# Queries of three more pairs by seven products of halves, with key/value units, sums of the input and a reload placed anew

## The chip, the cores and the metric

The kernel runs on one core of one Trainium2 chip. The metric is the device time of one execution in microseconds (us), the median of three runs. The profile comes from one further execution, taken by the hardware profiler.

Names used below: PE is TensorE's matmul, PEld its weight load, DVE is VectorE, ACT is ScalarE, POOL is GpSimd and SP is SyncE, whose queue issues nearly all transfers ("SPq"). In the trace every float32 matmul of the program appears as two records, so counts of records are twice the counts of matmuls in the code.

## The reference, cut to what matters

One layer over a sequence of S = 1024 tokens of width H = 512, all in float32, between two residual additions:

```python
# attention: 32 query heads, 8 key/value heads (groups), head size 128, causal
x = x + layernorm(attn(layernorm(x)))          # q, k, v, o projections, softmax over keys
# second half: dense 512 -> 512 with bias, plus 8 low-rank experts of rank 16
x = x + layernorm(ffn(layernorm(x)))           # router of 15 outputs, top 8, softmax weights
```

In `attn`, `q = xn @ w_q` has 4096 columns, that is 8 groups of 4 heads, and `k = xn @ w_k` and `v = xn @ w_v` have 1024 columns each, one head for each group. The changed lines concern `q`, and the places of `k` and `v`, for the last two of the eight groups.

## The kernel before

**Blocks.** The tokens are cut into 8 tiles of 128. A block (g, t) is the attention of one group g (four heads) for the queries of tile t; there are 64 blocks, numbered i = 0 to 63. Two consecutive blocks with tiles 2u and 2u+1 form a pair (g, u). Groups 0 to 5 take pairs 0 to 23 in order (blocks 0 to 47; the constant `N2` is 48). The last two groups are interleaved: pairs 24 to 31 are (6,0), (7,0), (6,3), (7,3), (6,2), (7,2), (6,1), (7,1), so blocks 48 to 53 are (6,0), (6,1), (7,0), (7,1), (6,6), (6,7), and block 54 is (7,6). A tile is finished once its block of group 7 is done; then come the output's norm, the router and the second half for that tile.

**One block.** The main loop goes through i. In each block `scores` runs four times (n = 0 to 3), each time on 128 rows (four heads of 32 queries): PE multiplies queries by keys into a PSUM tile `s` (a pool of two), DVE adds the mask (L618) and takes the negative maximum (L620), ACT takes the exponential into `p` (L625), DVE the reciprocal of the sum (L631), ACT scales `p` (L632), DVE transposes it in 32x32 squares into `T` (L638), and at the block's end SP issues 16 transfers from `T` to `K` (L109). Two blocks later `weighted_values` multiplies `K` by the values (`po`), and ACT copies the result to `attnT` (L669). After each of the four `scores` a quarter of the other matmul work of the block is emitted by `run_share`. That work is put together in `projections` and in the loop from: the queries of the next pair (`pq`), keys (`pk`), values (`pv` in the trace; in the loop the name `pv` holds the `po` pieces of block i-2), and the output projection of a finished pair by seven products (`pa` to `pe`), whose sums DVE adds up (L744). `weave` mixes two lists in proportion to their columns.

PE's order is the order in which the loop emits matmuls, since `keep` pins it; so one matmul that waits holds back all behind it. DVE, ACT, POOL and SP also work through queues in order.

**Queries in two ways.** `project_q` (L425 for its two copies by ACT) makes a pair's queries, 512 columns of `w_q` by 256 tokens, by 16 matmuls of 256 columns. `project_q_halves` makes the same by the seven products of a 2x2 scheme: the weights and the normed input `xnT` are cut into quarters, sums of quarters are made beforehand, and 28 matmuls of 128 columns follow, four for each product. The products lie in four PSUM banks (0 to 3, two products each, the last with one) and are put together by one ACT copy (L476) and six DVE additions (L450). Matmul banks come from a pool of three, so each bank must be emptied before the third bank after it is begun.

The sums are POOL's. `combine_q` (L145) makes four sums of quarters of `w_q` for one group, each 128x512, one of them in place in the weights, the others into three tiles tagged `hy`. `combine_x` (L188) makes four sums of quarters of `xnT` for one 256-token unit u, each 128x256, into two tiles tagged `x`, a pool of two: the sums of the next unit can't be written before the last matmul that reads the old ones. The same two buffers hold `xr`, the rows of x which `reload_x` brings back for the residual.

`QW` lists the pairs whose queries are made by halves: 2 to 24 before. Pairs 25 to 31 use `project_q`. The query weights of the last pairs alternate between groups 6 and 7 and have one buffer for each half (tags `wq0` and `wq1`), so at each even block `loads` issues two transfers of 512 KB on SP for the pair whose queries follow.

**Keys and values of the last two groups.** `project_k_halves` and `project_v_halves` make the keys and values of both groups for one unit u, 14 matmuls of 128 columns each. Unit 0 is made in block 47, units 1, 2 and 3 in blocks 49, 50 and 51 (n = 1, 2, 3 in `projections`). The keys are emitted ahead of the queries, the values go to `other`, which the loop weaves with the output projection and the values' products.

Of the kernel before, what the change touches and what calls it, by code (L numbers as in the profile page):

```python
# [22 lines left out]
def kernel(  # L23
# [36 lines left out]
    G = w_k.shape[1] // D  # L60
    R = w_q.shape[1] // D // G
    NT = S // P
# [6 lines left out]
    NSUB = P // SQ  # L69
    GV = 2  # L70
# [19 lines left out]
    blocks = [(g, 2 * u + e) for g, u in pairs for e in range(2)]  # L90
    N = len(blocks)
    N2 = (G - 2) * NT
    QW = range(2, N2 // 2 + 1)

    def keep(ins):
        return tc.keep_in_program_order(ins)
# [174 lines left out]
    def prepare_map():  # L271

        emap_f = const.tile([P, NR], F32, tag="emap_f", name="emap_f")
        keep(nc.vector.tensor_copy(emap_f, emap_i))
        for e in range(E):
            keep(
                nc.vector.tensor_scalar(
                    mexp[:, e, :], emap_f, float(e), SCALING, ALU.is_equal, ALU.mult
                )
            )  # L280
# [171 lines left out]
    def project_q_halves(m):  # L452


        g, u = pairs[m]
        hk = KC // 2
        pm = {}

        def half(e, h):

            return both(e)[:, h]

        def both(e):
            q = qTs[g, u][:, ts(e, NSUB), :, :]
            return q.rearrange("p s (x h) q -> p x s (h q)", x=2)

        def each(x):

            return qTs[g, u].rearrange("p s (x h) q -> p x s (h q)", x=2)[:, x]

        def merge(b):

            one, two = pm[b][:, 0], pm[b][:, 1]
            if b == 0:
                q = each(0).rearrange("p (e s) n -> p e s n", e=2)
                nc.scalar.copy(q, one.unsqueeze(1).to_broadcast([P, 2, NSUB, 2 * SQ]))  # L476
                add(half(0, 0), two, half(0, 0))
            elif b == 1:
                add(half(1, 0), one, half(1, 0))
                add(half(1, 1), two, half(1, 0))  # L480
            elif b == 2:
                add(half(0, 1), one, half(1, 1))
                add(half(1, 0), two, half(1, 0))
            else:
                add(both(1), one.unsqueeze(1).to_broadcast([P, 2, NSUB, 2 * SQ]), both(1))

        def piece(n, c, k):
            i, b, x = PRODUCTS[n], n // 2, n % 2
            if n == c == k == 0:
                qTs[g, u] = act.tile([P, PQ // SQ, R, SQ], F32, tag="qT", name=f"qT_{g}_{u}")  # L490
            if x == c == k == 0:
                whole = bank(f"pq_{g}_{u}_{b}")
                pm[b] = whole.rearrange("p (x s n) -> p x s n", x=2, s=NSUB)
            assert weights["sq"] == (g,) and weights["tx of"] == u
            matmul(
                pm[b][:, x, :, ts(c, SQ)],
                weights["sq", 0][i][:, k, ts(c, D)],
                weights["tx"][i][:, k, :].rearrange("p (s q) -> p s q", q=SQ),
                start=(k == 0),
                stop=(k == hk - 1),  # L500
            )
            if c == 1 and k == hk - 1 and (x == 1 or n == 6):
                merge(b)

        return [
            (P, lambda n=n, c=c, k=k: piece(n, c, k))
            for n in range(7)
            for c in range(2)
            for k in range(hk)
        ]  # L510
# [34 lines left out]
    def project_k_halves(g, u):  # L545
        def quarters():
            qb, at = u * PQ // QB, u * PQ % QB
            if at == 0:
                for n in (g, g + 1):
                    key_tile(n, qb)  # L550
            one, two = (kTs[n, qb][:, at : at + PQ] for n in (g, g + 1))
            return one[:, :P], one[:, P:], two[:, :P], two[:, P:], one.rearrange("p (e n) -> p e n", e=2)

        return project_halves(f"k{g}", u, ("sk", g), lambda w, x: (w, x), quarters)

    def project_v_halves(gv, u):
        def quarters():
            v = value_tile(gv, u)
            return v[:, 0, 0], v[:, 1, 0], v[:, 0, 1], v[:, 1, 1], v[:, :, 0]

        return project_halves(f"v{gv}", u, ("sv", gv), lambda w, x: (x, w), quarters)
# [204 lines left out]
    def reload_x(t):  # L766
        xt = state["x", t] = ffn.tile([P, H], F32, tag="x", name=f"xr_{t}")
        load(xt, x[ts(t, P), :])
# [118 lines left out]
    def projections(i):  # L887


        g, t = blocks[i]  # L890
        q, other = [], []
        m = i // 2 + 1
        if i == 0:
            later["q"] = project_q(*pairs[m])
            q = later["q"][: 2 * KC]
        elif i == 1:
            q = later["q"][2 * KC :]
        elif i % 2 and m < len(pairs):
            q = project_q_halves(m) if m in QW else project_q(*pairs[m])
        first = GV  # L900
        n = i - N2
        if i % 2 and m < len(pairs) and n < 0:
            gm, um = pairs[m]
            if gm >= first and gm % 2 == 0:
                q = project_k_halves(gm, um) + q + project_v_halves(gm // GV, um)
        if n < 0:
            if g < first and t == 2:
                other += project_k(g, 1)
            if g + 1 < first and t == 6:
                other += project_k(g + 1, 0)  # L910
            if g == 0 and t < 2:
                other += [(P * KC, lambda n=TPB + 2 + t: input_turn(n))]
                other += project_v(0, 2 + t)
            elif g == 0 and t >= TPB:
                other += project_v(0, t)
        elif 0 < n < NT // 2:
            q = project_k_halves(G - 2, n) + q
            other += project_v_halves((G - 2) // GV, n)
        return q, other

    def loads(i):
# [44 lines left out]
    def weave(a, b):  # L966

        na, nb = sum(c for c, _ in a), sum(c for c, _ in b)
        merged, at, bt, b = [], 0, 0, list(b)
        for c, f in a:  # L970
            merged.append((c, f))
            at += c
            while b and (bt + b[0][0] / 2) * na <= at * nb:
                bt += b[0][0]
                merged.append(b.pop(0))
        return merged + b
# [23 lines left out]
    def complete(i, *behind):  # L1000


        for e in range(2):
            k = i - behind[e % len(behind)]
            if 0 <= k < N and k % 2 == e and blocks[k][0] == G - 1:
                return [blocks[k][1]]
        return []
# [4 lines left out]
    ready = []  # L1012
    for i in range(N):
        loads(i)
        for t in complete(i, 2):
            reload_x(t)
        q, other = projections(i)
        pv = attend(i - 2) if i >= 2 else []
        o, o_pair, ends, begins = [], [], [], []
        for t in complete(i, 3):  # L1020
            o = project_o(*blocks[i - 3])
        if i % 2 == 0 and i >= 4 and blocks[i - 4][0] < G - 1:
            o_pair = project_o_pair(*pairs[i // 2 - 2])
        for t in complete(i, 6, 7):
            ends = sum(ffn_out(t), [])
        for t in complete(i, 5):
            begins = ffn_router(t)

        rest = o + weave(o_pair, other + pv[:2] + begins[1:] + pv[2:])

        if i % 2 and i // 2 + 1 in QW and blocks[i][1] > 1 and i > 3:
            cut = len(rest) * 3 // 5
            q, rest = weave(q, rest[:cut]), rest[cut:]
        then = begins[:1] + q + ends[:-1] + rest[:4] + ends[-1:] + rest[4:]
        for n in range(NSUB):
            scores(*blocks[i], n)
            run_share(then, n, NSUB)
            m = i // 2 + 1
            if i % 2 == 0 and m in QW:
                if n == 0:  # L1040
                    combine_x(pairs[m][1], m)
                if n == 1:
                    combine_q(m)
            g, t = blocks[i]
            if g % 2 and g + 1 < G and n == 1:
                if t == 6:
                    combine_k(g + 1)
                if t == 7:
                    combine_v((g + 1) // GV)
            if n == NSUB - 1 and i in (N2, N2 + 1, N2 + 2):  # L1050
                combine_x(i - N2 + 1, 0)
        if i == 1:
            combine_o(0)
        if i == NT:
            prepare_ffn()
        if i == NT + 4:
            prepare_map()
        ready += complete(i, 7, 8)
        for t in [t for t in ready if ("done", t) in state]:
            ready.remove(t)  # L1060
            ffn_store(t)

        if i >= NT and blocks[i - 2][1] == 0 and blocks[i - 2][0] < G - 1:
            combine_o(blocks[i - 2][0])
# [77 lines left out]
```

## Time and profile before

| | |
|---|---|
| three runs, us | 1066.48, 1066.59, 1067.16 (median 1066.59) |
| profiled execution: own time, span, us | 1066.64, 1064.9 |
| busy: PE, DVE, ACT, POOL, us | 1046.5, 740.1, 480.7, 255.0 |
| granted TensorE clock | 0.996 |

The span runs from the first instruction to the last; the profiled execution's own time is 1.7 us longer. A block can be found in the trace by its first score matmul, whose columns grow with the tile and the quarter: block 48 begins at 740.77 us, 49 at 753.71, 50 at 775.15, 51 at 789.77, 52 at 806.05, 53 at 818.64 and 54 at 837.25. In the chain of waits, each line says which engine's work stood on the path that ended last.

### The profile page before, as it was taken

Reading aid. Unit: us, or ns where it says so; the run is one execution under the profiler, and the core shown is the slowest. Engines: PE = TensorE matmul, PEld = TensorE weight load, DVE = VectorE, ACT = ScalarE, POOL = GpSimd, SP = SyncE. Lnnn points to the kernel's source line nnn. Section 1 sums busy time; section 2 is a strip of 40 time slices with the busy share of each in tenths; the row PEclk is TensorE's granted clock in tenths of the full one; section 3 lists DMA queues with packets and bytes.
Section 4 is the critical chain, followed back from the end, with each engine's and each line's share of the span. In section 5 each row is a group of like instructions: output and inputs, shape, how many; then the busy total and the mean of one; then the engine's idle time right before and its main releaser. Section 6 shows DMA issues by size and latency. Waiting matters only on the chain.

```text
span 1064.9 us, 15423 instructions
## 1 busy us (share of the span) xinstructions
PE 1046.5 (98%) x4782; PEld 729.8 (69%) x4782; DVE 740.1 (70%) x1810; ACT 480.7 (45%) x965; POOL 255.0 (24%) x491
## 2 busy tenths in 40 slices
PE   9999999999999999999999999999999999999996
PEld 7766667767777676767777667767787566466553
DVE  4586657876687766877577776887457766576756
ACT  3655435553344534553245544554235554353421
POOL 2613125241131215241130313351130110111212
PEclk9999999999999999999999999999999999999998
DMA  5146352563125442463225352464523754444231
GB/s 188 34 115 149 70 121 70 150 154 86 27 56 154 104 108 72 115 158 79 61 50 131 102 125 61 127 160 109 129 66 104 183 143 111 125 110 106 69 84 40
DMA packets 78513, 111.99 MB, mean 105 GB/s; under 512 B 18176, under 2 KB 49920, under 8 KB 78432
## 3 DMA queue, kind: packets, MB, share of 16 engines
q1 hardware_dynamic: 74960, 105.71, 39.5%
q0 software_dynamic: 2096, 3.46, 1.4%
q10 hardware_dynamic: 1376, 1.84, 0.5%
q8 instruction: 39, 0.64, 0.3%
q14 instruction: 42, 0.34, 0.1%
HBM read 33.34 MB, written 2.10 MB: 33 GB/s over the span
## 4 chain that ended last, share of the span: by engine, by line
PE 90%; DVE 3%; SPq 3%; ACT 1%; DMA 1%; issue 1%; POOL 0%; POOLq 0%; DVEq 0%; ACTq 0%
PE po L103 22%; PE s L103 20%; PE pq L103 19%; PE pv L103 5%; PE pe L103 4%; PE pa L103 4%; PE pk L103 4%; PE pf L103 3%; PE pO L103 3%; SPq L109 3%; PE pc L103 2%; PE pb L103 2%; PE pd L103 2%; PE pl L103 1%; DMA wo<-in_w_o_dram 1%
## 5 line engine op out<-in xcount | busy, mean ns | idle before, releaser
L632 ACT ACTIVATE p<-p,rec 128x32 f32<-128x32 f32 (+31 forms) x256 | 188.3, 736 | 225.8 <-DVE rec L631 164.8
L103 PE MATMUL po<-K,v 128*128 128x512 f32 x576 | 280.3, 594 | 1.7 <-DMA wo<-in_w_o_dram 1.0
L103 PE MATMUL s<-kT,qT 128*128 128x512 f32 (+15 forms) x768 | 272.4, 463 | 1.4 <-ACT p L625 1.3
L625 ACT ACTIVATE p<-s,nmax 128x32 f32<-128x32 f32 (+31 forms) x256 | 179.5, 701 | 163.1 <-DVE nmax L620 147.2
L638 DVE STREAM_TRANSPOSE T<-p 128x128 f32<-128x128 f32 (+7 forms) x256 | 197.7, 774 | 52.5 <-ACT p L632 37.9
L103 PEld LDWEIGHTS s<-kT,qT 128*128 128x128 f32 x768 | 141.2, 190 | 118.2 <-issue 105.9
L620 DVE TENSOR_REDUCE nmax<-s 128x1 f32<-128x32 f32 (+31 forms) x256 | 180.2, 704 | 7.3
L103 PEld LDWEIGHTS po<-K,v 128*128 128x128 f32 x576 | 103.6, 190 | 61.7 <-issue 51.4
L623 POOL MEMSET p<- 128x96 f32 (+2 forms) x192 | 29.3, 157 | 423.2 <-DVE T L638 377.5
L618 DVE TENSOR_TENSOR s<-s,smask 128x32 f32<-128x32 f32 x256 | 48.0, 187 | 99.4 <-PE s L103 98.8
L103 PE MATMUL pq<-xnT,wq 128*128 128x128 f32 (+1 forms) x656 | 113.3, 321 | 0.0
L103 PEld LDWEIGHTS pq<-xnT,wq 128*128 128x128 f32 x656 | 99.5, 191 | 14.0 <-issue 7.2
L188 POOL TENSOR_TENSOR tx<-xnT 128x256 f32<-128x256 f32 x52 | 37.9, 729 | 209.8 <-PE pv L103 124.6
L450 DVE TENSOR_TENSOR qT<-pq,qT 128x256 f32<-128x256 f32 x138 | 62.0, 460 | 32.0 <-ACT qT L476 18.9
L669 ACT COPY attnT<-po 128x512 f32<-128x512 f32 x64 | 37.4, 584 | 76.5 <-PE po L103 76.3
L103 PE MATMUL pa<-wo,attnT 128*128 128x256 f32 x224 | 58.8, 385 | 0.0
L103 PEld LDWEIGHTS pq<-tx,wq 128*128 128x128 f32 x368 | 47.1, 192 | 7.6 <-issue 7.5
L103 PEld LDWEIGHTS pq<-tx,sq 128*128 128x128 f32 x368 | 47.5, 192 | 5.7 <-issue 5.0
L103 PE MATMUL pq<-tx,sq 128*128 128x128 f32 x368 | 51.2, 275 | 0.0
L103 PEld LDWEIGHTS pa<-wo,attnT 128*128 128x128 f32 x224 | 41.0, 190 | 14.0 <-issue 9.3
L625 ACT ACTIVATION_READ_ACCUMULATOR p<-s,nmax 128x1 f32 x256 | 49.5, 193 | 0.0
L103 PE MATMUL pq<-tx,wq 128*128 128x128 f32 x368 | 49.2, 275 | 0.0
(146 smaller groups left out, 1258.4 us busy)
## 6 DMA issues: line engine op xcount, KB each, us to landing
K<-T SPq DMA_DIRECT2D x128, 128.0 KB, 2.4
K<-T SPq DMA_DIRECT2D x128, 112.0 KB, 2.3
wq<-in_w_q_dram SPq DMA_DIRECT2D x27, 512.0 KB, 4.8
K<-T SPq DMA_DIRECT2D x128, 96.0 KB, 2.2
K<-T SPq DMA_DIRECT2D x128, 80.0 KB, 2.1
wo<-in_w_o_dram SPq DMA_DIRECT2D x32, 256.0 KB, 3.9
K<-T SPq DMA_DIRECT2D x108, 64.0 KB, 2.0
K<-T SPq DMA_DIRECT2D x113, 48.0 KB, 2.0
```

The costliest lines, as they stand in the source:

```text
L103: keep(nc.tensor.matmul(*args, **kw))
L109: keep(by.dma_start(dst, src))
L188: nc.gpsimd.tensor_tensor(dst, p, q, ALU.subtract)
L450: nc.vector.tensor_tensor(dst, src, to, ALU.add)
L618: keep(nc.vector.tensor_tensor(s[:, n - SQ : n], s[:, n - SQ : n], smask, ALU.add))
L620: keep(nc.vector.tensor_reduce(nmax, s[:, :n], AX.X, ALU.max, negate=True))
L623: nc.gpsimd.memset(p[:, n:full], 0.0)
L625: keep(nc.scalar.activation(p[:, :n], s[:, :n], AF.Exp, bias=nmax, accum_out=total))
L632: keep(nc.scalar.mul(p[:, :n], p[:, :n], rec))
L638: nc.vector.transpose(turned[g, t][:, :, j, :, :].rearrange("p b k q -> p k b q"), p[:, :full].rearrange("p (k b q) -> p k b q", b=R, q=SQ),)
L669: copy = nc.scalar.copy(o, po)
```

## The change

`QW` is extended by three, to pairs 25, 26 and 27, which are (7,0), (6,3) and (7,3). Each of these needs sums of its weights, so `combine_q` now runs in blocks 48, 50 and 52, after the first quarter (n = 0) and not after the second.

The queries of pair 25 move from block 49 to block 48, and those of pair 27 from block 53 to block 52. In both blocks they stand at the end, behind the woven output projection and `po` work. Those of pair 26 stay in block 51. The sums of `xnT` of units 2 and 3 are emitted a quarter earlier. The keys and values of unit 1 stand in block 49 behind the first three `po` pieces, and those of units 2 and 3 stand ahead of the other work, the values no longer woven with the output projection. `reload_x`, and with it its transfer on SP, comes at the end of a block and not at its beginning. The query weights' transfers stay in the same blocks.

```diff
-    QW = range(2, N2 // 2 + 1)
+    QW = range(2, N2 // 2 + 4)
...
-        elif i % 2 and m < len(pairs):
+        elif i % 2 and m < len(pairs) and i not in (N2 + 1, N2 + 5):
             q = project_q_halves(m) if m in QW else project_q(*pairs[m])
...
         elif 0 < n < NT // 2:
-            q = project_k_halves(G - 2, n) + q
-            other += project_v_halves((G - 2) // GV, n)
+            kv = project_k_halves(G - 2, n), project_v_halves((G - 2) // GV, n)
+            if n == 1:
+                other += kv[0] + kv[1]
+            else:
+                q = kv[0] + q + kv[1]
+        elif n in (0, NT // 2):
+
+            other += project_q_halves(m)
         return q, other
...
         loads(i)
-        for t in complete(i, 2):
-            reload_x(t)
         q, other = projections(i)
...
         rest = o + weave(o_pair, other + pv[:2] + begins[1:] + pv[2:])
+        if i in (N2, N2 + NT // 2):
+            rest = weave(o_pair, pv) + other
+        if i == N2 + 1:
+            rest = pv[:3] + other + pv[3:]
...
             if i % 2 == 0 and m in QW:
-                if n == 0:
+                if n == 0 and i < N2:
                     combine_x(pairs[m][1], m)
-                if n == 1:
+                if n == (1 if i < N2 else 0):
                     combine_q(m)
...
-            if n == NSUB - 1 and i in (N2, N2 + 1, N2 + 2):
+            if (i, n) in ((N2, 3), (N2 + 1, 2), (N2 + 2, 2)):
                 combine_x(i - N2 + 1, 0)
...
+        for t in complete(i, 2):
+            reload_x(t)
         ready += complete(i, 7, 8)
```

## The prediction

> **What bounds the kernel now.** I read the page first. PE is busy for nearly the whole span and carries nine tenths of the chain that ended last.
>
> ```profile
> span 1064.9 us, 15423 instructions
> PE 1046.5 (98%) x4782; PEld 729.8 (69%) x4782; DVE 740.1 (70%) x1810; ACT 480.7 (45%) x965; POOL 255.0 (24%) x491
> ...
> PE 90%; DVE 3%; SPq 3%; ACT 1%; DMA 1%; issue 1%; POOL 0%; POOLq 0%; DVEq 0%; ACTq 0%
> ```
>
> So time is PE time plus whatever PE waits. Then I read PE's timeline over blocks 47 to 54 (start, length, engine, line, operation, count, and in brackets a wait). The first three lines are parts of the pair-24 products by halves (block 47), the next four the queries of pair 25 by full matmuls (block 49), the last the only wait of blocks 48 to 54.
>
> ```profile
> 730.70 1.06 PE L103 MATMUL pq<-xnT,sq 128*128 128x128 f32 x8
> 731.60 1.06 PE L103 MATMUL pq<-tx,sq 128*128 128x128 f32 x8
> 732.49 1.06 PE L103 MATMUL pv<-wv,xnT 128*128 128x128 f32 x8
> ...
> 757.11 1.89 PE L103 MATMUL pq<-xnT,wq 128*128 128x256 f32 x8
> 758.84 0.49 PE L103 MATMUL s<-kT,qT 128*128 128x192 f32 x2
> 759.16 5.34 PE L103 MATMUL pq<-xnT,wq 128*128 128x256 f32 x24
> 764.34 0.54 PE L103 MATMUL s<-kT,qT 128*128 128x224 f32 x2
> ...
> 784.22 0.49 PE L103 MATMUL pv<-wv,tx 128*128 128x128 f32 x2 [0.30 <-DVE acc L744]
> ```
>
> Lengths overlap, so cost is start to start: eight 128-column records take 0.89 us (731.60 to 732.49), 0.1115 each; 256-column records take 6.91 us for 32 (757.11 to 758.84 and 759.16 to 764.34), 0.216 each. The table of stretches gives each block's length and DVE's load in it; these are blocks 50, 52 and 53.
>
> ```profile
> 775.15:789.77 14.62, 14.32 (x96) 12.77 (x95) 10.38 (x36) 4.71 (x16) 3.20 (x7) 1.00 0.15 36
> ...
> 806.05:818.64 12.59, 12.59 (x47) 8.74 (x46) 11.25 (x23) 7.46 (x12) 0.30 (x2) 1.00 0.37 118
> 818.64:837.25 18.61, 18.61 (x62) 11.40 (x61) 14.19 (x22) 11.27 (x17) 0.61 (x4) 1.00 0.59 135
> ```
>
> Columns are length, then PE, PEld, DVE, ACT, POOL busy. POOL's and SP's timelines last: one set of weight sums takes 5.1 us, and SP's 16 transfers of a block stand 10 us ahead of the next weights.
>
> ```profile
> 706.17 1.27 POOL L145 TENSOR_TENSOR sq<-wq 128x512 f32<-128x512 f32 x1 [0.96 <-DMA wq<-in_w_q_dram]
> ...
> 709.98 1.27 POOL L145 TENSOR_TENSOR sq<-wq,sq 128x512 f32<-128x512 f32 x1
> ```
>
> ```profile
> 791.57 10.35 SPq L109 DMA_DIRECT2D K<-T  x16
> 802.02 1.08 SPq L109 DMA_DIRECT2D wq<-in_w_q_dram  x2
> ```
>
> [...] 0.1115 us for 128 columns against half of 0.216 for 256, 3% dearer per column. Seven products save 1/8 of the columns, so most of it should survive. [...] The trace's L450 rows have 415 and 686, which I use.
>
> **The change, part by part.**
>
> *Products.* Each pair loses 32 records of 0.216 (6.91 us) and gains 56 of 0.1115 (6.24 us; the 56 records of pair 24 sum to that too). Gain 0.67, three times: 2.0 us.
>
> *Block 50 unwoven.* Its parts, taken where they run unmixed: keys 3.12, values 3.12 (block 49, 28 records each), 14 output-projection matmuls at 0.432 make 6.05, `po` 0.86, scores 0.14+0.17+0.22+0.22: 13.9 us. Measured 14.62. The 0.3 wait and 0.4 of alternation may go: gain 0.7 if all goes, 0 if the new order only moves the wait.
>
> *DVE and ACT.* A pair drops two ACT copies of 0.59 and gets one (0.59) and additions of 5 x 0.415 + 0.69 = 2.8 us on DVE. Hidden behind PE if DVE keeps up; see rival 2.
>
> *Weights and their sums.* SP gets no new transfer. I place each against PE, with on before's clock. The new block lengths follow from the rows: 48 gains 6.24 (12.94 to 19.2), 49 loses 6.91 (21.44 to 14.5), 50 is 13.9, 51 loses 0.67 (16.28 to 15.6), 52 gains 6.24 (12.59 to 18.8), 53 loses 6.91 (18.61 to 11.7). So 49 begins at 759.9, 50 at 774.4, 51 at 788.3, 52 at 803.9, 53 at 822.7, 54 at 834.4, that is 2.8 earlier than before at the end.
> Pair 25: weights issued at 732.0, landed about 738 (4.8 us); sums 5.1, done by 744, queued on POOL only behind two memsets, since the unit-1 sums now come later. Its products start at 753. Nine us of room.
> Unit 1's sums must wait for pair 25's last product (same `x` buffers): 0.73 each, t2 ready at 761.5, all at 762.9. PE reaches t2 after a score, three `po` and four key matmuls, at 763.7. Room about 2 us. Without those three `po` (2.6 us) PE would wait near 0.4.
> `po` of block 47, now at 760 and not 768, needs K: 16 issues from 745.8, landed by 758.5. Room 1.5.
> Pair 26: 16 K issues of block 48 now begin near 761.5, weights issued at 772, landed 777, sums by 782.5, unit 3's sums by 786; used from 790. POOL's memsets behind them are needed at 784 or later.
> Pair 27: K of block 50 issued to 800.3, weights landed 806, sums by 811.4 (memset of the second score in front). Products begin where block 52 has done 11.1 us of other work: 815.0, first weight sum at 816.8. Room 5 us.
> `xr` on SP now waits for pair 27's last product (822.7) and stands in front of nothing until block 52's K issues at 826.9; `po` of block 52 needs these landed by 840.7, they land at 839.4. Room 1.3. The second `xr` and the weights of pair 28 go behind; needed ten us later.
> *Banks.* Pair 27's last bank needs the first emptied: 818 against 821.7. Pair 25 and 26 have as much.
>
> Sum: -2.0 -0.7 = -2.7; I leave 0.2 for small waits: -2.5. The profiled execution had 1066.64 (span 1064.9 and 1.7 around it), the median is 1066.59; so 1064.1, span about 1062.4. A measurement tells 0.2%, 2.1 us, from no change: 1064.46 is the border, and the forecast lies just beyond it.
>
> **Rivals.**
>
> 1. *Likeliest, chance 0.52:* all waits hidden, block 50 relieved wholly or mostly. 1063.8 to 1064.6.
>
> 2. *DVE takes PE's place in blocks 52 and 53, 0.22; the other sign.* Without the queries, block 53 has four score tiles with only 5.2 us of other work (six 512-column matmuls at 0.86). DVE was busy 25.4 of 31.2 us there, and gets 2.8 more: 28.2 against PE's new 30.5. If the 5.8 us in which DVE stood idle all remained (waits within the chain mask, maximum, exponential, reciprocal, scaling, transpose), 34.0 would be needed: a wait of 3.5 on scores for ACT's exponential, and 1066.6 - 2.7 + 3.5 = 1067.4, slower. It decides when over 2.7 us of it comes. For it: DVE had hardly a gap from 809.9 to 823 in block 52. Against it: following the chain tile by tile, each score's PSUM buffer is free 1.1 to 1.7 us before PE wants it, and the waits before came mostly from PE not having scores ready. Half of it gives 1065.7.
>
> 3. *Block 50 gives nothing, 0.18:* its additions on DVE are the same, and the wait reappears at another bank. 1066.6 - 2.0 = 1064.6, within the border.
>
> 4. *An operand comes late, 0.08:* weights of pair 27 or K of block 52. The room of 5 and 1.3 us goes first, then each us late is a us lost. Weights at 8.1 us (the page's slowest landing, at the start) for 4.8 would still be covered; K two us later would cost 0.7: 1064.8. For a loss overall K must be late by 4.
>
> That the change does not do what it says is out: the changed program's order shows 84 new product matmuls in place of 48.
>
> **How the numbers follow.** Rival 1 falls beyond the border in about nine of ten, rival 2 in one of five (1063.9 to 1067.4, likely 1065), rival 3 in one of four, rival 4 in four of ten. Faster: 0.47+0.04+0.04+0.03 = 0.58. Slower by 2.1 us (1068.7) needs rival 2 at its full size and a late operand as well, or something unseen: 0.08. Same: 0.34. The range 1063.5 to 1066.2 leaves out a gain above 3.1 (nothing supports it beyond the sum) and the upper half of rival 2. The likeliest case's own range is 1063.8 to 1064.6.
>
> **What would show it.** Steps right: PE's timeline has 56 records of 128 columns, 6.2 us of start-to-start time, at the end of blocks 48 and 52 and within 51; 256-column `pq` records fall from 288 to 192; block 48 is near 19.2 us long, 49 near 14.5, 50 near 13.9, 52 near 18.8, 53 near 11.7; no wait above 0.3 in them. Wrong: `s` waiting for ACT L625 in block 53 (rival 2), `pv` or a bank waiting for DVE in 50 (rival 3), `pq` waiting for POOL `sq` in 52, or `po` for K in 54 (rival 4). A step from POOL in block 49, `pk` waiting for `tx`, would show the unit-1 sums mistimed. It all goes wrong if a 128-column record costs more beside these neighbours than in block 47: at 0.123 each the whole saving of the products is gone.

## The result, and the profile after

The changed kernel took 1064.36 us in the median (1062.69 to 1065.39), the kernel before 1066.52 beside it (1065.54 to 1067.72). The ratio is 0.9978, with a 95% interval of 0.9970 to 0.9987: faster, by 2.2 us where 2.5 were forecast, and just beyond the 2.1 us that the prediction took as the border of what can be told. Both are medians of 13 executions; of the changed kernel's, three ran at a mean granted clock of 0.995 and took 1064.70 to 1065.33 us, the other ten (0.996 to 0.998) have a median of 1063.9, and no execution of the kernel before that stands beside the experiments is below 0.996.

The profiled execution took 1063.05 us, its span is 1061.3. First the page of the kernel after: the span, the busy times, and the shares of the chain of waits.

```profile
span 1061.3 us, 15618 instructions
PE 1044.3 (98%) x4854; PEld 730.7 (69%) x4854; DVE 748.8 (71%) x1828; ACT 478.2 (45%) x962; POOL 269.4 (25%) x503
...
PE 93%; DVE 3%; SPq 1%; ACT 1%; DMA 1%; issue 1%; POOL 0%; POOLq 0%; DVEq 0%; ACTq 0%
```

PE has 2.2 us less work in 72 more records, DVE 8.7 us more (three pairs' additions are 8.3 of it), and the chain is still PE's. Next the table of stretches of the kernel after, one line for each of blocks 48 to 54: the stretch and its length, then PE, PEld, DVE, ACT and POOL busy with their instruction counts, the granted clock, DMA share and GB/s.

```profile
739.55:758.75 19.20, 19.20 (x108) 15.13 (x107) 11.91 (x30) 5.31 (x15) 3.97 (x7) 1.00 0.50 110
758.75:773.28 14.53, 14.53 (x83) 10.65 (x82) 8.34 (x30) 4.41 (x14) 4.47 (x8) 1.00 0.10 22
773.28:787.32 14.04, 14.04 (x95) 12.85 (x94) 10.69 (x36) 4.90 (x16) 8.20 (x12) 1.00 0.37 106
787.32:802.95 15.63, 15.63 (x125) 14.62 (x124) 10.50 (x35) 5.07 (x15) 5.47 (x7) 1.00 0.39 114
802.95:821.80 18.85, 18.85 (x103) 14.99 (x102) 15.64 (x29) 9.26 (x15) 5.41 (x7) 1.00 0.34 96
821.80:833.50 11.70, 11.70 (x31) 5.33 (x29) 10.62 (x19) 7.50 (x10) 0.30 (x2) 1.00 0.41 97
833.50:848.63 15.13, 15.13 (x39) 7.22 (x38) 14.69 (x30) 9.72 (x15) 3.34 (x7) 1.00 0.92 226
```

In each line PE's busy time equals the length, and PE's waits of this run name none in these seven blocks. Against before (us, from each block's first score to the next block's):

| block | before | forecast | after |
|---|---|---|---|
| 48 | 12.94 | 19.2 | 19.20 |
| 49 | 21.44 | 14.5 | 14.53 |
| 50 | 14.62 | 13.9 | 14.04 |
| 51 | 16.28 | 15.6 | 15.63 |
| 52 | 12.59 | 18.8 | 18.85 |
| 53 | 18.61 | 11.7 | 11.70 |
| sum | 96.48 | 93.7 | 93.95 |

The change gains 2.53 us in these six blocks. The two profiled spans differ by 3.6, and most of the rest arose before the first changed instruction: block 48 starts at 739.55 and not at 740.77, though each engine's instructions up to there are the same. PE's timeline of the kernel before has three waits for transfers ahead of block 48:

```profile
150.78 3.67 PE L103 MATMUL po<-K,v 128*128 128x512 f32 x8 [0.50 <-DMA K<-T]
...
328.27 1.10 PE L103 MATMUL po<-K,v 128*128 128x512 f32 x2 [0.55 <-DMA wo<-in_w_o_dram]
...
573.86 1.10 PE L103 MATMUL po<-K,v 128*128 128x512 f32 x2 [0.49 <-DMA wo<-in_w_o_dram]
```

PE's timeline of the kernel after has one:

```profile
327.35 1.10 PE L103 MATMUL po<-K,v 128*128 128x512 f32 x2 [0.30 <-DMA wo<-in_w_o_dram]
```

1.54 against 0.30 us accounts for that difference of 1.2, to within smaller waits elsewhere. In the profiles of the runs below, block 48 starts anywhere from 739.5 to 740.8. So a single execution says little about 2 us, and the lengths of blocks 48 to 62, which repeat to 0.03 us from profile to profile where an edit leaves them alone, say much.

PE's timeline of the kernel after shows the last 40 of pair 25's 56 records, at the end of block 48; the last line is the first score of block 49:

```profile
754.28 1.06 PE L103 MATMUL pq<-tx,sq 128*128 128x128 f32 x8
755.17 1.95 PE L103 MATMUL pq<-tx,wq 128*128 128x128 f32 x16
756.96 1.06 PE L103 MATMUL pq<-xnT,sq 128*128 128x128 f32 x8
757.85 1.06 PE L103 MATMUL pq<-tx,sq 128*128 128x128 f32 x8
758.75 0.44 PE L103 MATMUL s<-kT,qT 128*128 128x160 f32 x2
```

From 754.28 to 758.75 they take 4.47 us, 0.112 each. `pq` records of 256 columns fell from 288 to 192.

### The profile page after: what moved, and what is told of

It is laid out like the page before. It is cut to its first block, busy times and chain, and to the rows that moved or that the text cites. A ratio compares the mean times of both kernels' runs of the same rounds, so it can differ in the third digit from the quotient of the medians.

```text
span 1061.3 us, 15618 instructions
## 1 busy us (share of the span) xinstructions
PE 1044.3 (98%) x4854; PEld 730.7 (69%) x4854; DVE 748.8 (71%) x1828; ACT 478.2 (45%) x962; POOL 269.4 (25%) x503
## 4 chain that ended last, share of the span: by engine, by line
PE 93%; DVE 3%; SPq 1%; ACT 1%; DMA 1%; issue 1%; POOL 0%; POOLq 0%; DVEq 0%; ACTq 0%
PE po L103 23%; PE s L103 21%; PE pq L103 19%; PE pv L103 5%; PE pk L103 5%; PE pe L103 4%; PE pa L103 4%; PE pf L103 3%; PE pO L103 3%; PE pc L103 2%; PE pb L103 2%; PE pd L103 2%; SPq L109 1%; PE pl L103 1%; DVE T L638 1%
## 5 line engine op out<-in xcount | busy, mean ns | idle before, releaser
L103 PE MATMUL pq<-xnT,wq 128*128 128x128 f32 (+1 forms) x608 | 97.5, 308 | 0.0
L103 PEld LDWEIGHTS pq<-xnT,wq 128*128 128x128 f32 x608 | 87.5, 191 | 11.3 <-issue 6.6
L450 DVE TENSOR_TENSOR qT<-pq,qT 128x256 f32<-128x256 f32 x156 | 69.9, 461 | 35.8 <-ACT qT L476 19.8
L103 PEld LDWEIGHTS pq<-tx,wq 128*128 128x128 f32 x416 | 53.0, 192 | 7.9 <-issue 7.5
L103 PE MATMUL pq<-tx,sq 128*128 128x128 f32 x416 | 57.5, 275 | 0.0
L103 PEld LDWEIGHTS pq<-tx,sq 128*128 128x128 f32 x416 | 53.4, 192 | 5.7 <-issue 5.0
L103 PE MATMUL pq<-tx,wq 128*128 128x128 f32 x416 | 55.4, 275 | 0.0
```

Of the source, the lines that this page charges most:

```text
L103: keep(nc.tensor.matmul(*args, **kw))
L450: nc.vector.tensor_tensor(dst, src, to, ALU.add)
```

## The experiments

Two theories stood after this. A room, here as in the prediction, is the time by which an operand or a buffer is ready before PE wants it. The first theory: each part has its own gain in PE records (0.65 for each pair, 0.58 for block 50) and the rest hides in the rooms. The second: the gain needs the placing, since at least one of the rooms is nearly used up. Lengths of blocks are in us; times carry their ratio to the kernel before.

**Pair 27 by full matmuls, in its old block and in its new one.** Two kernels, the changed one with pair 27 taken out of the products:

```diff
-    QW = range(2, N2 // 2 + 4)
+    QW = range(2, N2 // 2 + 3)
...
-        elif i % 2 and m < len(pairs) and i not in (N2 + 1, N2 + 5):
+        elif i % 2 and m < len(pairs) and i != N2 + 1:
...
-        elif n in (0, NT // 2):
+        elif n == 0:
```

> The changed kernel with pair 27 alone put back: full matmuls in block 53, no weight sums for it. If the products are the gain (my theory): blocks 52 and 53 together last 31.2 us as before, against 30.55 in the changed kernel (0.67 for one pair), and no wait appears; the time lies about 1.5 us below the kernel before. If placing the queries of pair 27 in block 52 matters by itself (rival), 52 and 53 together differ from 31.2 by more than 0.2.

The second has only the first of these edits, and `project_q(*pairs[m])` in the place of block 52's products.

> As the run before, but the full matmuls of pair 27 stand at the end of block 52, where the changed kernel has its products. Theory (products alone gain): block 52 19.5 us, block 53 11.7, together 31.2, no wait. Rival (the thinned block 53 costs by itself, VectorE being the limit): over 31.2 together, with a wait of the scores for ScalarE's exponential in block 53.

Measured: 1064.07 us, 0.9979 (0.9970 to 0.9987), blocks 52 and 53 are 12.60 and 18.60; and 1064.08, 0.9976 (0.9966 to 0.9987), blocks 19.50 and 11.70. Both sum to 31.20, without a wait, and after has 30.55. So the pair's products gain 0.65 and moving full matmuls gains nothing; the times themselves can't tell 0.65.

**Block 50's values alone.** The kernel before, with the values of unit 2 behind its keys:

```diff
-            other += project_v_halves((G - 2) // GV, n)
+            kv = project_v_halves((G - 2) // GV, n)
+            if n == 2:
+                q += kv
+            else:
+                other += kv
```

> The kernel before with one edit: in block 50 the values of unit 2 stand behind its keys and are no longer woven with the output projection. Theory: block 50 goes from 14.62 to 14.0, the wait for VectorE of 0.3 goes, time 0.6 below the kernel before. Rival (the wait moves to another bank): 14.6 and no gain.

Measured: 1065.32, ratio 0.9992 (0.9985 to 0.9998); block 50 went from 14.62 to 14.05, the other blocks didn't change, and the wait of 0.30 for DVE L744 is gone. The gain is there without any other edit: 0.30 is the wait, and the remaining 0.27 went with the alternation.

**Pair 26 alone.** The kernel before with one pair more by products, and nothing else moved. (The early return in `combine_q` is kept for the earlier pairs only.)

```diff
-    QW = range(2, N2 // 2 + 1)
+    QW = [*range(2, N2 // 2 + 1), N2 // 2 + 2]
...
-                if n == 0:
+                if n == 0 and i < N2:
                     combine_x(pairs[m][1], m)
```

> The kernel before with pair 26 alone (block 51) by seven products. Theory (0.67 us for each pair, independent of the other edits): block 51 is 15.6 us long for 16.28, the others as before, 1065.8 us or a ratio near 0.9994. Rival (the products gain only together with the other edits, since the sums of weights or of xn come late where nothing else is moved): a wait of pq for the sums in block 51, no gain.

Measured: 1067.64, ratio 1.0019 (1.0011 to 1.0026), slower by 1.7 us. Block 51 is 15.63, as the theory says, but block 50 grew from 14.62 to 16.54, where neither theory nor rival had put anything; the two together show 1.3 of the loss. PE's timeline of this run names the place:

```profile
780.03 0.46 PE L103 MATMUL pv<-wv,xnT 128*128 128x128 f32 x2 [1.74 <-ACT p L625]
```

The first values of block 50 had no bank, as I read it: the pool has three, the two banks of the keys and that of `pa` were in use, and the keys' are emptied by additions on DVE (L450). The releaser named, ACT's exponential, is only the last event that the profile shows, so DVE's timeline of this run has to be read as well:

```profile
775.00 1.48 DVE L720 TENSOR_TENSOR sums<-attnT 128x256 f32<-128x256 f32 x1 [2.81 <-ACT attnT L669]
776.51 1.37 DVE L721 TENSOR_TENSOR sums<-sums,attnT 128x256 f32<-128x256 f32 x1
777.81 0.41 DVE L722 TENSOR_TENSOR attnT<-attnT,attnT 128x256 f32<-128x256 f32 x1
...
778.64 0.41 DVE L450 TENSOR_TENSOR kT<-pk,kT 128x256 f32<-128x256 f32 x1
```

L720 and L721 are the same additions as L722, and take three times as long. POOL's timeline of this run shows what stood beside them:

```profile
773.70 1.27 POOL L145 TENSOR_TENSOR sq<-sq,wq 128x512 f32<-128x512 f32 x1
774.93 1.27 POOL L145 TENSOR_TENSOR wq<-wq,wq 128x512 f32<-128x512 f32 x1
776.15 1.45 POOL L145 TENSOR_TENSOR sq<-wq,sq 128x512 f32<-128x512 f32 x1
```

L720 ends 0.3 us after the second of these lines ends, and L721 0.3 after the third: each seems to have waited for a sum of weights. L722 began behind the last of the sums and took 0.41. Not every addition on DVE grew so: in the kernel after, a sum of pair 26 (POOL, 778.90 to 780.17) runs beside `v` additions of products out of PSUM, and two of these, of 128x256, take 0.75 us there (779.24); in the next run two take 0.73 (782.82) with no sum beside them. Why the one kind grows and the other doesn't is not shown.

**The same, with the sums a quarter later.** If the two additions are the cause, moving POOL's sums past them should give everything back:

```diff
-                if n == 1:
+                if n == (1 if i < N2 else 2):
                     combine_q(m)
```

> The kernel before with pair 26 alone by seven products, as in the run p26_alone, but its sums of weights start behind the third share of block 50 and not behind the second: about 779.5 us instead of 772.4. Theory ([...] in p26_alone L720 and L721 took 1.48 and 1.37 us instead of 0.42, which made the key additions 1.9 us late and PE wait 1.74 for a bank): L720 and L721 are back at 0.42, the wait of 1.74 is gone, block 50 is about 14.6 us and block 51 15.63; the time is 1.9 below p26_alone, 1065.7 us or a ratio near 0.9996. Rival (the sums of weights cost wherever they stand in block 50, through GpSimd's order ahead of the sums of xn for unit 3, or through other additions on VectorE): block 50 stays near 16.5 us, or PE waits for sums in block 51, about 1067.6 us.

Measured: 1065.47, ratio 0.9993 (0.9985 to 1.0002); block 50 is 14.62 again, block 51 15.63. DVE's timeline of this run:

```profile
774.70 0.43 DVE L720 TENSOR_TENSOR sums<-attnT 128x256 f32<-128x256 f32 x1 [2.81 <-ACT attnT L669]
775.16 0.42 DVE L721 TENSOR_TENSOR sums<-sums,attnT 128x256 f32<-128x256 f32 x1
```

The sums now start at 777.55 us, by chance the same time as in the changed kernel, which starts them after an earlier quarter but whose weights are issued later. 1.92 us of block 50 hung on where four POOL instructions stood. In the changed kernel one addition took longer in this way beside the new sums of weights, in block 48, where such a sum runs on POOL from 740.35 to 741.61. DVE's timeline has it:

```profile
740.37 1.52 DVE L720 TENSOR_TENSOR sums<-attnT 128x256 f32<-128x256 f32 x1 [1.55 <-ACT attnT L669]
```

There it costs nothing: block 48 is 19.20 long, as forecast, and PE has no wait in it.

**Unit 1's keys and values ahead of the three `po` pieces** (changed kernel):

```diff
-            rest = pv[:3] + other + pv[3:]
+            rest = other + pv
```

> The changed kernel with the keys and values of unit 1 first in block 49, ahead of all po work and not behind three pieces of it. As I worked it out in the prediction: PE waits about 0.4 us at pk for GpSimd's sums of unit 1. As the trace of the changed kernel suggests (the buffer of t1 and t2 came free 1.5 us earlier than I had it): no wait, block 49 stays at 14.5.

Measured: 1064.08, ratio 0.9980 (0.9971 to 0.9988). Block 49 is 14.53, with no wait. The wait of 0.4 that the prediction had put there doesn't exist. POOL's timeline of the kernel after says why:

```profile
757.21 0.73 POOL L188 TENSOR_TENSOR tx<-xnT 128x256 f32<-128x256 f32 x1 [3.25 <-PE pq L103]
...
758.99 0.73 POOL L188 TENSOR_TENSOR tx<-xnT 128x256 f32<-128x256 f32 x1 [0.25 <-PE pq L103]
```

The four sums lie in two buffers, and the first buffer came free at 757.2 while PE was still at pair 25's products, 1.8 us ahead of the second. All four were done at 760.4, or 761.6 on before's clock, where the prediction had 762.9.

**DVE's room in blocks 52 to 54**, measured with transposes of scores done twice (the repeat writes the same values). Each of these two kernels ran once, so only its blocks are compared. First two transposes of block 53, 2.5 us more of DVE:

```diff
-            pin(
-                nc.vector.transpose(
+            for _ in range(2 if blocks.index((g, t)) == N2 + 5 and j < 2 else 1):
+                pin(
+                    nc.vector.transpose(
```

> The changed kernel with two more VectorE instructions: the transposes of the first two score tiles of block 53 are done twice (1.23 us each, 2.5 in all; the result is the same). Room theory: in the changed kernel the exponentials of block 53 and 54 end 1.2 to 2.1 us before PE wants their buffers, so 2.5 us on VectorE show as a wait of only 0.2 to 0.5 at the scores. Rival 2 at full force (VectorE is already the limit there): a wait of about 2.5. No link: none.

Then five, the last of block 52 and all of block 53, 6.0 us more:

> The same with five transposes doubled: the last of block 52 and all four of block 53 (1.1 + 4 x 1.23 = 6.0 us more on VectorE). Room theory: the room is used up, waits of the scores for ScalarE's exponential of 2 to 2.5 us in blocks 53 to 55, or later. Rival 2 at full force: 6. No link: none.

Measured: with two, 1063.08 us; blocks 53 and 54 are 11.70 and 15.13, as in after, and there is no wait, not even the 0.2 to 0.5 expected. With five, 1065.39; block 53 is 11.75, block 54 17.38. The waits are on PE's timeline of the run with five:

```profile
838.20 1.66 PE L103 MATMUL s<-kT,qT 128*128 128x512 f32 x4 [0.28 <-ACT p L625]
839.70 1.02 PE L103 MATMUL pO<-wo,attnT 128*128 128x512 f32 x2
841.07 1.10 PE L103 MATMUL po<-K,v 128*128 128x512 f32 x2 [0.34 <-issue]
842.64 1.72 PE L103 MATMUL s<-kT,qT 128*128 128x512 f32 x4 [0.48 <-ACT p L625]
```

The two waits for ACT are rival 2's, at rival 2's row, one block later than it said. The one between them is a `po` that waits for K: the doubled transpose of block 52 delays K's sixteen issues, which end at 838.92 in this run, and 2.15 us behind them, the time from such issues to `po` that a run further down shows, is 841.07. 6.0 us cost 2.3: between 2.5 and some 3.7 us more of DVE work were still free after the change (an estimate, since a part of the loss came through K). (A bracket counts from the end that the profile models for the record before, so the three make only 1.1; the whole loss shows in the distances of the starts.)

**Pair 27's sums late.** The first of its weight sums repeated eight times ahead of the real one, 10.7 us of POOL (the repeats are overwritten by the same sum; `late` is set for pair 27 alone):

```diff
+        for _ in range(8 if weights.get("late") else 0):
+            keep(nc.gpsimd.tensor_tensor(s1, a21, a22, ALU.add))
```

> The changed kernel with the first of pair 27's four weight sums made eight times more on GpSimd (8 x 1.27 = 10.2 us; the result is the same), so that they end 10.2 us later. By the prediction's room of 5 us PE waits 5.2 at the first product that needs a sum, in block 52. By the changed kernel's trace (second sum done at 809.7, wanted at 815.8) the room is 6.1 and the wait 4.1 to 4.4. If the small fills of p that queue behind them on GpSimd hold VectorE's transposes as well, more than that.

Measured, in one execution: 1072.19 us, block 52 26.68, that is 7.8 longer and not 4 to 5. PE's timeline of this run:

```profile
822.18 2.08 PE L103 MATMUL pq<-tx,sq 128*128 128x128 f32 x8 [4.92 <-POOL sq L147]
824.05 0.64 PE L103 MATMUL pq<-tx,wq 128*128 128x128 f32 x2
824.48 3.19 PE L103 MATMUL s<-kT,qT 128*128 128x512 f32 x4
```

The wait is of the kind expected, and its 4.9 us lie between the 4.1 to 4.4 and the 5.2 of the two readings. But eight records behind it take 1.87 us and not 0.89, and the score 2.99 and not 1.50. The stretches of this run say why; the third number from the end is the granted clock:

```profile
818.00:820.00 2.00, 0.00 (x0) 0.00 (x0) 1.68 (x3) 0.19 (x2) 1.92 (x2) 1.00 0.13 33
820.00:822.00 2.00, 0.00 (x0) 0.00 (x0) 0.00 (x0) 0.85 (x1) 1.98 (x3) 0.71 0.00 0
822.00:824.00 2.00, 1.82 (x8) 1.82 (x9) 0.00 (x0) 0.00 (x0) 2.00 (x3) 0.50 0.00 0
824.00:826.00 2.00, 2.00 (x6) 1.16 (x5) 0.00 (x0) 0.00 (x0) 0.70 (x2) 0.50 0.00 0
826.00:828.00 2.00, 2.00 (x7) 1.21 (x6) 0.25 (x2) 0.00 (x0) 0.00 (x0) 0.59 0.00 0
828.00:831.00 3.00, 3.00 (x29) 3.00 (x28) 2.86 (x5) 1.10 (x2) 0.15 (x1) 1.00 0.20 35
```

The clock fell during the wait: with 0.71 as the mean of 820 to 822, between stretches of 1.00 and 0.50, it was at a half from about 820.8 on, 3.7 us behind the end of PE's work at 817.1. It returned during the work: 0.59 as the mean of 826 to 828, between 0.50 and 1.00, puts that near 827.6, some 5.5 us behind the first matmul (both estimates take the clock as either 1.00 or 0.50). Counted from start to start, the wait took 5.08 us (817.10 to 822.18) and the slower records 2.75, half of those 5.5: together the 7.83 that block 52 grew.

**Pair 27's products in block 53** (changed kernel):

```diff
-        elif i % 2 and m < len(pairs) and i not in (N2 + 1, N2 + 5):
+        elif i % 2 and m < len(pairs) and i != N2 + 1:
...
-        elif n in (0, NT // 2):
+        elif n == 0:
```

> The changed kernel with the products of pair 27 in block 53 and not at the end of block 52. Products theory: block 52 12.6, block 53 17.9, together 30.5 as in the changed kernel, so the place gains nothing by itself; a small wait (up to 0.5) in block 54, since the reload of x now waits on SP for these products, and the transfers of block 52's K stand behind it. Rival (the place in block 52 is what makes it fast): over 1 us longer.

Measured: 1065.14, ratio 0.9991 (0.9982 to 1.0000). Blocks 52 and 53 are 12.60 and 17.95, together 30.55 as in after; but block 54 is 15.92 for 15.13, somewhat more than the 0.5 expected. SP's timeline of this run, and then PE's:

```profile
828.08 0.33 SPq L109 DMA_DIRECT2D xr<-in_x_dram  x1
828.53 10.99 SPq L109 DMA_DIRECT2D K<-T  x16
```

```profile
841.67 1.10 PE L103 MATMUL po<-K,v 128*128 128x512 f32 x2 [0.49 <-DMA K<-T]
```

`xr` waits for the products, because it is written where their sums lie, and holds the sixteen K transfers behind it, though DVE had the last of block 52 in `T` by 822.35: they begin 6.3 us ahead of block 54 (which starts at 834.79 here), and 7.5 ahead in after (825.96, 833.50). So what the move to block 52 gives is not in PE's records; it keeps SP free, and saves 0.8 us.

**More pairs.** Since the rooms hold, three further pairs in blocks 57, 59 and 61, with their sums laid over parts of `xnT` that nothing reads any more (the lines with `over` are for these pairs alone):

```diff
-    QW = range(2, N2 // 2 + 4)
+    QW = [*range(2, N2 // 2 + 4), 29, 30, 31]
...
+            over = xnT[1][:, :, ts(1, PQ)]
+            last = ffn.tile([P, hk, 2 * D], F32, tag="skv", name=f"sq_{m}", bufs=1)
+            sums = [over[:, :hk], over[:, hk:], last]
...
+            over = xnT[0][:, :, ts(0, PQ)]
+            t1, t2, t3, t4 = over[:, :hk, :P], over[:, :hk, P:], over[:, hk:, :P], over[:, hk:, P:]
...
-                if n == 0 and i < N2:
+                if n == 0 and (i < N2 or m in (29, 30)):
                     combine_x(pairs[m][1], m)
-                if n == (1 if i < N2 else 0):
+                if n == (1 if i < N2 else 0 if m < 28 else 2):
                     combine_q(m)
```

> The changed kernel with three more pairs (29, 30 and 31, in blocks 57, 59 and 61) by seven products of halves; their sums of weights and of xn lie over parts of xnT that nothing reads any more. Theory (PE's records set the time, everything else is hidden while the rooms hold): each of blocks 57, 59 and 61 is 0.67 us shorter than in the changed kernel, 2.0 in all, so about 1062.3 us. Rival (VectorE has too little room in the last blocks, and 2.8 us more additions for each pair are not hidden): PE waits for scores or for sums of xn in or behind these blocks, one of them gives its 0.67 back or loses up to 2, so 1063 to 1066 us.

Measured: 1061.90, ratio 0.9963 (0.9951 to 0.9976), 4.0 us below the kernel before, and faster than the changed kernel by the medians (which come from different sets of runs; the intervals overlap by 0.0006). The blocks, start to start, are 21.39 for 22.04 (57), 17.67 for 18.31 (59) and 18.08 for 18.60 (61): 1.8 of 2.0 us, with no listed wait in them. The profile also has a wait of 0.91 for K in block 63, which is 62.67 long for 62.23 in after; the run with four pairs doesn't have it, so whether it belongs to the added pairs is open.

A fourth, pair 28, has its sums and products in blocks 54 and 55, where DVE is nearly full (the same code, with 28 in the list and `combine_x` for 28 and 30):

> The kernel with pairs 29, 30 and 31 by halves too, and pair 28 (block 55) besides. Theory of the rooms: VectorE is busy 14.56 of 15.0 us in block 54, where pair 28's sums of xn (2.8 us with the additions behind the products) would come, and its weights land only near 843.5 us, 6 us ahead of the products, against 5.1 us of sums on GpSimd; so this pair gives nothing or costs: block 55 is no more than 0.67 shorter, and waits of 0.5 to 2 us stand in blocks 55 to 57. About 1062.3 to 1064.5 us. Rival (records alone count): 0.67 less again, about 1061.6 us and no wait.

Measured: 1065.26 (1062.55 to 1068.44), ratio 0.9992 (0.9986 to 0.9999). That is 3.4 us above the kernel with three, where between 0.7 less and some 2 more was expected. The profiled execution has one wait in blocks 48 to 62, on PE's timeline:

```profile
851.60 1.06 PE L103 MATMUL pq<-xnT,wq 128*128 128x128 f32 x8
854.44 1.10 PE L103 MATMUL po<-K,v 128*128 128x512 f32 x2 [1.78 <-DMA K<-T]
```

It is not the wait for DVE or POOL that I had expected. The products are woven with the `po` pieces, the full matmuls weren't, so block 55's first `po` now comes at 852.5 us and not near 861, while K's sixteen transfers are issued until 852.3. Block 55 is 23.10 long, not 21.74. Whether DVE's room would have been enough stays open: this wait comes first.

Block 55 makes 1.4 us of the loss. Of the rest, the stretches of this run show a part in block 63, which is 63.89 long for 62.23 in after:

```profile
1012.00:1014.00 2.00, 1.63 (x4) 1.38 (x5) 1.47 (x4) 0.00 (x0) 0.00 (x0) 0.61 0.20 49
1014.00:1016.00 2.00, 2.00 (x4) 0.86 (x4) 0.96 (x3) 0.61 (x1) 0.00 (x0) 0.54 0.00 0
```

The granted clock, third from the end again, was a half for about 3.4 us here (an estimate from 0.61 and 0.54, again with 1.00 or 0.50 alone). The four `pc` and eight `pf` records take 6.06 us from start to start, and 4.37 in after. PE's waits just ahead are 1.25 us for DVE and 0.47, as in after, where the clock stayed at 1.00 (1008 to 1020 us): so here it fell behind waits much shorter than the 5.08 us of the run with late sums. The times of the other executions fall apart in the same way: eleven with a mean clock of 0.994 or 0.995 took 1065.26 to 1068.44 us, ten with 0.996 or 0.997 took 1062.55 to 1064.72. So about 2 us of the wide spread go with the clock (the medians of the two groups are 1065.88 and 1063.92). Whether the fourth pair brings its fall about isn't shown; none of the five executions with three pairs is below 0.996.

## Why the prediction was right

**Products.** 0.67 for each pair was forecast; blocks 48 and 49 lost 0.65, block 51 0.65, blocks 52 and 53 0.65. A 128-column record costs the same beside these neighbours: 0.112 us each at the end of block 48, 0.1115 in block 47. Run by run the term also held alone (pair 26 in block 51, pair 27 taken out). (Of the three lines that the prediction shows for block 47, the last is of values; it only closes the interval of 0.89.)

**Block 50 unwoven.** 0.7 forecast if all goes, 0.58 measured, and it goes alone as well (14.05). Rival 3 falls: the wait didn't come back at another bank. The 0.2 kept for small waits was not needed as such; it happened to cover these two terms, which were a little too large. That the blocks' 2.53 meets the forecast 2.5 so closely is luck to that extent.

**DVE and ACT, and rival 2.** Hidden, as forecast. Blocks 52 and 53 hold 26.3 us of DVE where before had 25.4; most of the pair's work slid into block 54 (12.0 to 14.6 in its first 15.0 us). The step of rival 2 that failed is that the 5.8 us of DVE's idle time would all remain: the dose of 2.5 us, which went in without a wait on top of the pair's own work, shows that much of it was slack. Its row was right, and its place but for one block, and 2.3 us are lost when 6.0 more are added. What it left out is block 54, where DVE is now busy for 14.69 of 15.13 us.

**Weights and their sums.** Pair 27's room was 6.1 us, not 5 (second sum done at 809.7, wanted at 815.8). The late run bears this out: there the second sum ended 11.2 us later than in after, counted from block 48's start, and PE lost 5.1 waiting, which leaves 6.1. Rival 4's rule, that each us late is a us lost, is wrong in size for a long wait: 4.9 cost 7.8. Unit 1's room was mis-sized too, through the step "unit 1's sums must wait for pair 25's last product": the buffers came free one by one. So the three `po` ahead of the keys protect nothing.

K of block 52 was the closest. The prediction gave it 1.3 us of room, with landing at 839.4 and `po` at 840.7. The sixteen issues ended at 837.26 in the trace of after. In the run with pair 27 in block 53, the `po` that waited for K began 2.15 us behind the end of K's issues (839.52 to 841.67); the same here gives 839.4, for a `po` at 839.67, so the room was near 0.3 us (an estimate). What was mis-sized is the time of the issues: the prediction allowed 12.5 us from the first issue (826.9) to the last landing (839.4), and by the same estimate it took 13.4 here, since the issues alone took 11.3, where this block's took 10.26 in before.

**What the prediction had no step for**: that additions on DVE may take longer beside POOL's new sums (L720 1.48 us for 0.43). It priced the sums' ends against PE's products, and DVE's work by its undisturbed durations. The kernel before already had the sign, in blocks 20 and 36; this is block 20, on DVE's and on POOL's timeline:

```profile
311.18 0.86 DVE L720 TENSOR_TENSOR sums<-attnT 128x256 f32<-128x256 f32 x1 [0.47 <-ACT attnT L669]
```

```profile
311.04 0.73 POOL L188 TENSOR_TENSOR tx<-xnT,tx 128x256 f32<-128x256 f32 x1
```

In its new places the changed kernel met it only where it cost nothing; with pair 26 alone, 2.0 us of it on DVE cost more than the pair gained. In the changed kernel the weights of pair 26 landed only at 777.5 us, when these additions had ended at 775.65. So in this point the forecast was right by luck: it had not weighed these times against each other.

## What to carry to other kernels

When work is added to POOL, compare its place with that of the additions on DVE, and follow what is queued behind these up to a PSUM bank: a sum that is in time for its own reader can still stop PE through somebody else's bank. Here two additions took 1.48 and 1.37 us beside sums of weights, for 0.43 and 0.42, and PE waited 1.74. Judge a change of 0.2% by the lengths of the blocks it touches, which repeated here to 0.03 us, while whole executions of one kernel differed by more than 2 us; and read the granted clock beside the times before a spread is put down to waits. And when products are put in place of a plain matmul, look at what the weaving pulls forward with them.

## What was not expected of the hardware

- A PE wait of 4.9 us cost 7.8, through a clock of 0.50 for about 5.5 us behind it (an estimate from the stretches); with pair 28 the mean clock was 0.61 and 0.54 in two stretches of 2 us, behind waits of only 1.25 and 0.47 us.
- VectorE's additions into `sums` (L720 and L721, 128x256) took 1.37 to 1.52 us beside GpSimd's sums of weights, and 0.43 and 0.42 with these sums a quarter later; with pair 26 alone the two of them delayed VectorE by 2.0 us in block 50, and PE waited 1.74.
- The same instructions reached block 48 at 739.5 to 740.8 us in the profiles here. Between before and after the difference lies in waits of 0.3 to 0.55 us for transfers of K and `wo`, which stand in one execution and not, or shorter, in the other.
